# One transfer per tile for B and C of the small Mamba in a two-layer metaformer kernel

## The chip, the cores and the metric

The kernel runs on one core of one Trainium2 chip. The metric is the device time of one execution in microseconds (us). A version's time is the median of several executions.

## The reference, cut to what matters

The input is 8 images of 256 channels and 32 x 32 pixels, so 1,024 tokens each. Two layers follow one another: a large Mamba block and a mixture of experts, then a block of depthwise convolutions with a small Mamba, and a feed-forward on the best half of the tokens.

```python
# layer 0
x = x + vim_block(ln_c(x))            # Mamba, 512 inner channels, 16 states
t = t + moe(ln_t(t))                  # 8 experts, the best 2 of each token
# layer 1
x_mb = x[:, 224:256]                  # 32 channels go to the small Mamba
x = x + concat(x_id, conv3x3, conv1x11, conv11x1, mamba(x_mb))
t = t + ffn_on_top_half(ln_t(t))
```

The small Mamba has 64 inner channels and 16 states for each image. With u, delta, B and C computed from the tokens, it runs along the 1,024 tokens:

```python
dA  = exp(delta[..., None] * A)                       # A: 64 channels x 16 states
dBu = delta[..., None] * B[:, :, None, :] * u[..., None]
h = h * dA_t + dBu_t                                  # for each token t
y = sum(h * C_t[:, None, :], axis=-1)
```

B and C have one value for each image, token and state. They are the same for all 64 channels of an image, and differ between images.

## The kernel before, in words

**Tiling.** Channels lie on the 128 partitions, tokens on the free axis, in halves of N = 512 tokens. The large Mamba has 512 inner channels, so four blocks of 128; it runs as 16 units (8 images by 2 halves of the tokens). The small Mamba has only 64 channels, so two images share the partitions: image 0 of the pair has partitions 0 to 63, image 1 has 64 to 127. Eight images make four groups, and each group runs the small Mamba once (`mamba_in`, `mamba_scan`, `mamba_out`).

**One pair of states.** `scan_pair` (L777) does two states of one half for 128 channels, in this order: GpSimd multiplies delta times u by B of both states (L780, tile `dbu`); ScalarE makes the decay (L785); VectorE scans along the tokens (L788) and multiplies by C (L793); where a pair is marked, GpSimd adds the two states (L797); TensorE adds the products into the accumulator `y` (L804). The large Mamba needs 512 such pairs in all, the small one 64 (4 groups by 8 pairs of states by 2 halves).

**B and C.** For each pair, B of two states is one tile `bc` of 128 partitions x 2 x 512 f32 (512 KB), and C is another. There are four `bc` buffers for both Mambas (`"bc": tiles("bc", wide2, 4)`, L467), taken strictly in the order of the planned priorities. A buffer is free again once its reader has gone: L780 for B, the second L793 for C. The values come from a DRAM tile `rows`. In the large Mamba (L839) one DMA on SyncE's queue spreads two rows over all 128 partitions. In the small Mamba the two images need different rows: `rows` of one half has 64 rows of 512 values, first 32 for image 0 (16 of B, 16 of C), then 32 for image 1. The function `fetch` (L1413) therefore issues two DMAs for one tile, one for each image and half of the partitions.

**What sets the order.** Nothing runs in the order of the source. Each piece of work is a `Step` with an engine, an estimated cost and a priority. `Flow.run` (L206) is a list scheduler that runs while the program is built: it simulates the engines with these costs, picks steps by priority, and so fixes the order of the instructions on each engine, SyncE's DMA queue too. Buffers are assigned as the plan reaches them. `dma` (L203) makes a step on SyncE of `us` microseconds (0.4 unless said otherwise) whose data comes 2.3 + KB/180 us later. On the chip each engine follows its fixed order and waits on semaphores only. While TensorE is expected to be idle, `warm` (L522) puts filler matmuls there (L525).

**Beside the small Mamba.** The small Mambas of groups 0 to 2 lie among the large Mamba's last units, experts of other groups, and the feed-forward. Their loads stand in the same queue: expert weights (L1127, `we`, three buffers), rows of experts (L1088, `xb`), stores (L1187), tokens in and out (L904, L1617, L1645).

Of the kernel before, what the change touches and what calls it, by code (L numbers as in the profile page):

```python
# [38 lines left out]
N = 512  # L39
KC = C // P  # L40
DI0, DI1, DS, DR0 = 512, 64, 16, 16
# [131 lines left out]
class Flow:  # L173
# [29 lines left out]
    def dma(self, prio, kb, run, reads=(), writes=(), fills=(), claims=(), us=0.4):  # L203
        return self.step(SP, us, prio, run, reads, writes, fills, claims, lat=2.3 + kb / 180)
# [94 lines left out]
def layers(g, ctx, x, a, out):  # L299
    tc, nc = g.tc, g.nc  # L300
# [142 lines left out]
    step, dma = flow.step, flow.dma  # L443
# [54 lines left out]
    def buf(name, line=None):  # L498
        b = Buf(pool[name], line)
        if line is not None:  # L500
            line.bufs.append(b)
        return b
# [270 lines left out]
    def paired(i, sp):  # L773

        return (sp + 1) * PAIRED[i] // (DS // 2) > sp * PAIRED[i] // (DS // 2)

    def scan_pair(prio, dts, dtxs, n, bt, ct, y, scales, initial, last, stop, paired):  # L777

        dbu = buf("dbu")
        gpsimd(2.45, prio, lambda: nc.gpsimd.tensor_tensor(  # L780
            dbu.v, dtxs.v[:, n : n + 1].to_broadcast(wide2), bt.v, ALU.mult), [dtxs, bt], [dbu], scan=True)
        for j in range(2):

            h = buf("da")
            step(ACT, 0.69, prio, lambda j=j, h=h: nc.scalar.activation(  # L785
                h.v, dts.v[:, n], AF.Exp, scale=scales(j)), [dts], [h], table="exp", scan=True)
            at = [] if initial is None else [initial[0]]
            step(DVE, 1.25, prio, lambda j=j, h=h: nc.vector.tensor_tensor_scan(  # L788
                h.v, h.v, dbu.v[:, j], 0.0 if initial is None else initial[1](j), ALU.mult, ALU.add),
                [dbu, *at], [h], scan=True)  # L790
            if last is not None:
                step(ACT, 0.19, prio, lambda j=j, h=h: nc.scalar.copy(last[1](j), h.v[:, N - 1 :]), [h], fills=[last[0]])  # L792
            step(DVE, 0.68, prio, lambda j=j, h=h: nc.vector.tensor_tensor(  # L793
                dbu.v[:, j], h.v, ct.v[:, j], ALU.mult), [h, ct], [dbu], scan=True)

        if paired:
            gpsimd(1.3, prio + 2.3, lambda: nc.gpsimd.tensor_tensor(  # L797
                dbu.v[:, 0], dbu.v[:, 0], dbu.v[:, 1], ALU.add), [], [dbu])

        def sums():  # L800
            if stop and n == 0:
                live[0] = None
            for j in range(1 if paired else 2):
                nc.tensor.matmul(  # L804
                    y.v[:, n], g.ident, dbu.v[:, j], start=False, stop=stop and (paired or j == 1)
                )

        step(PE, 0.9 if paired else 1.8, prio + 2.5, sums, [dbu], [y], scan=True)

    def start_y(y, skips, xs, prio):  # L810
        def go(n):
            nc.tensor.matmul(y.v[:, n], skips[n], xs.v[:, n], start=True, stop=False)
            if n == 0:
                live[0] = y

        for n in range(2):
            step(PE, 0.9, prio, lambda n=n: go(n), [xs], fills=[y])

    def end_y(y, sz, prio):
        for n in range(2):  # L820
            step(DVE, 0.72, prio, lambda n=n: nc.vector.tensor_tensor(
                sz.v[:, n], sz.v[:, n], y.v[:, n], ALU.mult), [y], [sz])
# [581 lines left out]
    def mamba_scan(n, pos):  # L1404
        grp = groups[n]
        state, y = buf("state1"), buf("y")
        start_y(y, [skip1, skip1], grp["xs"], pos)
        for sp in range(DS // 2):
            for hf in range(2):
                both = buf("bc"), buf("bc")  # L1410
                for j in range(2):

                    def fetch(j=j, hf=hf, sp=sp, both=both):  # L1413
                        for i in range(2):
                            at = i * 2 * DS + j * DS + 2 * sp
                            nc.sync.dma_start(
                                both[j].v[i * DI1 : (i + 1) * DI1],
                                grp["rows"][hf].v[at : at + 2].partition_broadcast(DI1),
                            )

                    dma(pos + 2 * sp + hf - 6, 512, fetch, [grp["rows"][hf]], [both[j]], us=0.8)
                scan_pair(
                    pos + 2 * sp + hf, grp["dt"], grp["dtx"], hf, *both, y,
                    lambda j, sp=sp: neg_a1[:, 2 * sp + j : 2 * sp + j + 1],
                    (state, lambda j, sp=sp: state.v[:, 2 * sp + j : 2 * sp + j + 1]) if hf else None,
                    None if hf else (state, lambda j, sp=sp: state.v[:, 2 * sp + j : 2 * sp + j + 1]),
                    sp == DS // 2 - 1, paired(len(units) + n, sp),
                )
        end_y(y, grp["sz"], pos + DS)
# [235 lines left out]
    for i, s in enumerate(UNIT_AT):  # L1665
        if i == 0:
            unit_prep(0)
        dt_of(i, 1, s + 4)
        if i + 1 < len(units):
            fetch_x(i + 1, s)  # L1670
        scan_unit(i, s)
        if i + 1 < len(units):
            unit_prep(i + 1)
        end = s + 2 * DS
        tokens(i, end + 1)
        if i % 4 == 3:
            n = i // 4
            at = PLAN[n]
            route(n, end + 12)
            scatter(n, end + 16, at["put"])  # L1680
            experts(n, *at["experts"])
            combine(n, *at["combine"])
            taps_of(n, *at["taps"])
            m = at["mamba"]
            mamba_in(n, m - 26, m + 5)
            mamba_scan(n, m)
            mamba_out(n, m + DS + 2)
            assemble(n, *at["assemble"])
            ranks(n, at["ranks"])
            feed_forward(n, *at["ffn"])  # L1690
            finish(n, *at["finish"])
# [146 lines left out]
```

## Time and profile before

| What | Value |
|---|---|
| median of 3 executions | 3852.95 us (3839.76 to 3853.16) |
| the profiled execution, its own time | 3870.05 us |
| span from first to last instruction | 3868.2 us, granted TensorE clock 0.940 |
| large Mamba's `bc` DMAs (L839) | 512, issued from 51.0 to 2874.4 us |
| small Mamba's `bc` DMAs (L1416) | 256, issued from 2328.9 to 3642.3 us |
| the four small Mambas, first to last L1416 issue | 2328.9 to 2430.0, 2856.8 to 2985.3, 3263.5 to 3378.6, 3535.6 to 3642.3 us |
| length of these four windows | 101.1, 128.5, 115.1, 106.7: 451.4 us |

An engine's busy time is the time in which it runs instructions. The DMA share is the mean share of time in which each of the core's 16 DMA engines had a packet in hand, and a packet here is mostly one run of up to 4,096 bytes into one partition. "L780 <- DMA bc<-rows" in a table of waits means that the instruction of line 780 had an idle engine before it until a transfer into `bc` had landed. DMA instructions on SyncE's queue (SPq) have a duration too, that of their issue, not of their transfer.

### The profile page before, as it was taken

What the parts mean: (1) busy time and instruction counts of PE and PEld (TensorE: products, weight loads), DVE (VectorE), ACT (ScalarE), POOL (GpSimd) and SP (SyncE); (2) the same over time, 40 slices, a digit from 0 to 9 for tenths busy, and PEclk for the clock granted to TensorE, in tenths of its full rate; (3) what the DMA queues carried; (4) which work ended last, traced back from release to release, by engine and by line L of the source; (5) the groups of instructions that cost most, each with busy time, mean ns of one, the idle gap of its engine ahead of it and who ended that gap; (6) DMA issues with size and microseconds to landing.
All of it is one profiled execution on the core that took longest, in us unless ns stands there. A gap on an engine that the chain in (4) does not pass through costs nothing. (4 is left out here: it accounts for less than half of the span.)

```text
span 3868.2 us, 38209 instructions
## 1 busy us (share of the span) xinstructions
PE 3299.0 (85%) x10818; PEld 1849.4 (48%) x10818; DVE 2978.3 (77%) x4281; ACT 2207.2 (57%) x4010; POOL 2327.8 (60%) x1587
## 2 busy tenths in 40 slices
PE   8888888788889888978997798988987889799768
PEld 3333333333544444434553444554555666566446
DVE  4899899989679978976898898779787527557751
ACT  4555565465757557645765665665764456556433
POOL 3567567588577768866775886545765433424522
PEclk9999999999999999998999999999888989899989
DMA  6333333344544435535553558654669666967955
GB/s 232 122 123 131 114 131 132 106 151 162 200 139 167 165 129 194 181 111 172 172 174 122 195 181 226 204 184 136 200 204 223 222 213 214 243 215 215 247 175 168
DMA packets 277073, 676.67 MB, mean 175 GB/s; under 512 B 33063, under 2 KB 114349, under 8 KB 276862
## 3 DMA queue, kind: packets, MB, share of 16 engines
q1 hardware_dynamic: 258430, 623.88, 51.2%
q0 software_dynamic: 18432, 50.36, 4.1%
q8 instruction: 87, 1.43, 0.2%
q14 instruction: 124, 1.02, 0.1%
HBM read 572.92 MB, written 101.19 MB: 174 GB/s over the span
## 5 line engine op out<-in xcount | busy, mean ns | idle before, releaser
L780 POOL TENSOR_TENSOR dbu<-dtx,bc 128x1024 f32<-128x1024 f32 x576 | 1359.3, 2368 | 515.6 <-PE y L804 349.0
L804 PE MATMUL y<-dbu,ident 128*128 128x512 f32 x1564 | 822.6, 635 | 217.9 <-POOL dbu L797 185.7
L785 ACT ACTIVATE mm<-dt,neg_a 128x512 f32<-128x512 f32 x1152 | 770.3, 688 | 208.2 <-DVE dbu L793 190.4
L788 DVE TENSOR_TENSOR_SCAN mm<-mm,dbu 128x512 f32<-128x512 f32 x576 | 703.9, 1222 | 229.7 <-ACT mm L785 153.8
L793 DVE TENSOR_TENSOR dbu<-mm,bc 128x512 f32<-128x512 f32 x1152 | 796.4, 691 | 81.4 <-DMA bc<-rows 18.0
L788 DVE TENSOR_TENSOR_SCAN mm<-mm,state,dbu 128x512 f32<-128x512 f32 x576 | 738.2, 1282 | 59.5 <-POOL dbu L780 38.7
L797 POOL TENSOR_TENSOR dbu<-dbu 128x512 f32<-128x512 f32 x370 | 480.9, 1301 | 299.4 <-DVE dbu L793 291.3
L804 PEld LDWEIGHTS y<-dbu,ident 128*128 128x128 f32 x1564 | 281.6, 197 | 560.5 <-POOL dbu L797 278.7
L1179 PE MATMUL mm<-we,hid 128*128 128x256 f32 x1984 | 486.4, 398 | 36.0 <-ACT state L792 13.0
L792 ACT COPY state<-mm 128x1 f32<-128x1 f32 x576 | 91.4, 160 | 731.6 <-DVE dbu L793 710.9
L1157 PE MATMUL mm<-xbt,we 128*128 128x256 f32 x1984 | 474.3, 391 | 30.4 <-DMA we<-in_W12f 10.4
L1179 PEld LDWEIGHTS mm<-we,hid 128*128 128x128 f32 x1984 | 387.8, 199 | 156.3 <-issue 47.4
L1157 PEld LDWEIGHTS mm<-xbt,we 128*128 128x128 f32 x1984 | 383.4, 196 | 139.2 <-issue 46.9
L525 PE MATMUL y<-still 128*128 128x512 bf16 x1059 | 275.7, 395 | 0.0
L721 PE MATMUL mm<-pre,w_tap 128*128 128x512 f32 (+3 forms) x512 | 240.8, 612 | 28.6 <-ACT pre L708 27.3
L440 ACT ACT_TABLE_LOAD x176 | 225.8, 1283 | 3.1
L1250 POOL DMA_INDIRECT ys<-slots_y,slot x128 | 122.2, 954 | 160.0 <-PE mm L1262 69.0
L1163 ACT ACTIVATE hid<-mm,we 128x256 f32<-128x256 f32 x496 | 196.8, 475 | 37.8 <-PE mm L1157 29.1
L525 PEld LDWEIGHTS <-still 128*128 128x128 bf16 x1059 | 105.9, 101 | 192.6 <-issue 118.8
L721 PEld LDWEIGHTS mm<-pre,w_tap 128*128 128x128 f32 x512 | 95.5, 193 | 166.8 <-issue 103.9
L1068 POOL DMA_INDIRECT slots_x<-xg,slot x128 | 129.8, 1014 | 68.4 <-DVE acc_b L1323 31.2
L1621 POOL DMA_INDIRECT ys<-y,slot_t x64 | 63.1, 986 | 158.7 <-DVE xc L1631 59.0
(251 smaller groups left out, 3983.6 us busy)
## 6 DMA issues: line engine op xcount, KB each, us to landing
bc<-rows SPq DMA_DIRECT2D x512, 512.0 KB
bc<-rows SPq DMA_DIRECT2D x256, 256.0 KB
we<-in_W SPq DMA_DIRECT2D x92, 514.0 KB
we<-in_W SPq DMA_DIRECT2D x92, 512.0 KB
xb<-slots_x SPq DMA_DIRECT2D x92, 256.0 KB
slots_y<-xo SPq DMA_DIRECT2D x92, 256.0 KB
we<-in_W12f SPq DMA_DIRECT2D x32, 514.0 KB
xc<-x SPq DMA_DIRECT2D x64, 256.0 KB
```

Source lines behind the costliest of these rows:

```text
L440: nc.scalar.preload_act_table_set(tables[name])
L525: nc.tensor.matmul(live[0].v[:, 0], still, wide, start=False, stop=False)
L721: nc.tensor.matmul(tc_.v[:, cut:], w_tap[:, c, j], pre.v[:, cut + j : j + N], start=j == 3, stop=j == 0)
L780: gpsimd(2.45, prio, lambda: nc.gpsimd.tensor_tensor(dbu.v, dtxs.v[:, n : n + 1].to_broadcast(wide2), bt.v, ALU.mult), [dtxs, bt], [dbu], ...
L785: step(ACT, 0.69, prio, lambda j=j, h=h: nc.scalar.activation(h.v, dts.v[:, n], AF.Exp, scale=scales(j)), [dts], [h], table="exp", scan=True)
L788: step(DVE, 1.25, prio, lambda j=j, h=h: nc.vector.tensor_tensor_scan(h.v, h.v, dbu.v[:, j], 0.0 if initial is None else initial[1](j), AL ...
L793: step(DVE, 0.68, prio, lambda j=j, h=h: nc.vector.tensor_tensor(dbu.v[:, j], h.v, ct.v[:, j], ALU.mult), [h, ct], [dbu], scan=True)
L797: gpsimd(1.3, prio + 2.3, lambda: nc.gpsimd.tensor_tensor(dbu.v[:, 0], dbu.v[:, 0], dbu.v[:, 1], ALU.add), [], [dbu])
L804: nc.tensor.matmul(y.v[:, n], g.ident, dbu.v[:, j], start=False, stop=stop and (paired or j == 1))
L1157: nc.tensor.matmul(tv[:, f], we[0].v[:, at : at + P], xbt.v[:, k], start=k == 0, stop=k == KC - 1)
L1163: nc.scalar.activation(hid.v[:, f], tv[:, f % 2], func, bias=we[0].v[:, at : at + 1])
L1179: nc.tensor.matmul(to, hid.v[:, f, h * P : (h + 1) * P], we[1].v[:, f * C : (f + 1) * C], start=extra is None and f == 0, stop=f == FC - 1,)
```

## The change

`fetch` issues one DMA per `bc` tile. Its source is a view of `rows` with a leading dimension of two images, then a dimension of 64 that repeats with step zero, then the two rows; its destination is the whole tile of 128 partitions. The estimated cost of the step falls from 0.8 to 0.4 us, so the planner sees the same bytes with a shorter issue. Nothing else is edited; what the lower estimate does to the order of the other instructions is the planner's doing.

```diff
                     def fetch(j=j, hf=hf, sp=sp, both=both):
-                        for i in range(2):
-                            at = i * 2 * DS + j * DS + 2 * sp
-                            nc.sync.dma_start(
-                                both[j].v[i * DI1 : (i + 1) * DI1],
-                                grp["rows"][hf].v[at : at + 2].partition_broadcast(DI1),
-                            )
-
-                    dma(pos + 2 * sp + hf - 6, 512, fetch, [grp["rows"][hf]], [both[j]], us=0.8)
+
+                        rows = grp["rows"][hf].v.rearrange("(i m) n -> i m n", i=2)
+                        at = j * DS + 2 * sp
+                        nc.sync.dma_start(
+                            both[j].v, rows[:, at : at + 2].unsqueeze(1).to_broadcast([2, DI1, 2, N]))
+
+                    dma(pos + 2 * sp + hf - 6, 512, fetch, [grp["rows"][hf]], [both[j]])
```

In the built program the new DMA has the destination pattern 128 partitions x 1 x 1,024 values and the source pattern 2 (step 32 rows) x 64 (step 0) x 1,024 values. Each old one had 64 partitions x 1,024 values on the destination and 64 (step 0) x 1,024 on the source. The new line is L1417.

## The prediction

> **What bounds the kernel now.** I began with the page's first two parts, to see whether one engine sets the time.
>
> ```profile
> span 3868.2 us, 38209 instructions
> ...
> PE 3299.0 (85%) x10818; PEld 1849.4 (48%) x10818; DVE 2978.3 (77%) x4281; ACT 2207.2 (57%) x4010; POOL 2327.8 (60%) x1587
> ```
>
> None does over the whole span: TensorE's 85% contains 1,059 filler matmuls (275.7 us at L525), and VectorE has 77%. So the change must be judged inside the four windows in which the small Mambas fetch B and C. The table by windows sets them beside a stretch of the large Mamba (200 to 400 us). Its columns are length, busy time of each engine, granted clock, DMA share, GB/s.
>
> ```profile
> core 0: us, PE busy (x) PEld busy (x) DVE busy (x) ACT busy (x) POOL busy (x), PEclk, DMA share, GB/s
> 200.00:400.00 200.00, 172.29 (x473) 76.34 (x473) 186.57 (x226) 106.85 (x173) 138.47 (x74) 0.95 0.39 129
> 2328.90:2430.00 101.10, 84.22 (x254) 44.04 (x253) 79.86 (x97) 57.73 (x96) 61.94 (x39) 0.95 0.85 216
> 2856.80:2985.30 128.50, 105.65 (x368) 71.30 (x365) 95.96 (x117) 66.07 (x118) 70.56 (x39) 0.88 0.86 220
> 3263.50:3378.60 115.10, 88.69 (x332) 62.90 (x331) 59.34 (x63) 68.96 (x117) 50.61 (x30) 0.90 1.01 247
> 3535.60:3642.30 106.70, 80.25 (x300) 48.49 (x298) 86.45 (x80) 66.30 (x115) 68.93 (x45) 0.92 0.98 264
> ```
>
> In the large Mamba VectorE is the bound (186.57 of 200 us) and the DMA engines are 39% busy. In the small Mamba's windows VectorE falls to 52 to 81%, and the DMA engines are 85 to 100% busy, at only 216 to 264 GB/s. The view of one source line says who waits for these transfers:
>
> ```profile
> L1416 SPq DMA_DIRECT2D bc<-rows x256: 444/498/995, 2328.9 to 3642.3; - x128
> ...
>   POOL dbu L780: 115.8, 35
>   DVE dbu L793: 18.0, 14
> ```
>
> GpSimd's multiply by B waited 115.8 us for them and VectorE's multiply by C 18.0 us, of 451.4 us of windows. So these windows are bound by DMA. The DMA view of the third window says how full the queue is:
>
> ```profile
> DMA packets 11236, 28.46 MB, mean 247 GB/s; under 512 B 1520, under 2 KB 5104, under 8 KB 11231
> ...
> q1 hardware_dynamic: 11039, 27.87, 99.6%
> ```
>
> 99.6% x 16 x 115.1 us over 27.87 MB is 15.2 bytes per ns and engine. In 200 to 400 us the same view has 38.5% for 25.75 MB: 20.9. In the trace's list of packets, those of 4,096 bytes take a median of 159 ns and a mean of 186 between 100 and 300 us. In the four windows their medians are 264 to 280 ns and their means 251 to 280 (together 263). The same bytes are slower when they go to half the partitions.
>
> [...] No view of the profile names the engine of a packet, and the trace of before has no transfer with such a mismatch. Its w_dt load of 17 rows (L345) does raise its semaphore in only two steps, at 4.25 and 10.43 us, where a tile of 128 rows shows 16[...].
>
> **The change part by part.**
>
> *Split over engines.* The old transfers have 64 on both sides[...]. The new source starts with 2 images, the new destination with 128 partitions. [...] each of two engines takes 64 packets, and the other 14 take none. I take this. The other bound is k = 16, a gain, worked out among the rivals.
>
> *Engine time of the two.* One tile is 64 packets x 159 ns = 10.2 us on each of the two engines. One small Mamba has 32 tiles: 325.6 us; all four 1,302 us. [...] I take the trace's undisturbed 159 ns with little on it: 165 ns, 1,352 us. Bounds: 156 ns, the shortest in the list for this size (1,278 us), and 186 ns, the large Mamba's mean (1,524 us).
>
> *What else stands on the two engines.* [...] In the order built from the changed kernel, between first and last L1417 issue of the four groups stand other SyncE transfers of 5.0, 10.0, 13.0 and 9.3 MB, 37.3 MB. A sixteenth is 2.33 MB, at 4,096 bytes per 159 ns 90 us.
>
> *Do the two engines ever run dry?* B's buffer returns after a multiply of 2.35 us (L780) and C's after about 2.7 us (L788 and L793 at 1.28 and 0.69 us, with waits), while three tiles or more, 30 us, are still queued. So the Mamba's own loop keeps them full. What can empty them is the work in between: an expert's weights land only when their sixteenth on the two slow engines has passed, up to 30 us later; ScalarE (L1163) and SyncE (L1127, L1187) wait for them or for what follows from them, and behind them in their fixed orders stand the exponentials of L785 and the next L1417. Before, the engines idled 15% of 101.1, 14% of 128.5 and 2% of 106.7 us, some 35 us. I keep this 35 us, since the same waits now lie beside longer transfers; bounds zero and a quarter more on the windows (360 us).
>
> *Sum.* The windows become 1,352 + 90 + 35 = 1,477 us instead of 451.4: +1,026 us. All other engines fit beneath: PE's busy time in the four windows is 358.8 us, VectorE's 321.6. Their order is fixed, so work after the windows cannot come forward to fill the 14 idle engines' time. Cover that I lean on: that other transfers of the windows, 90 us, add to the time and are not hidden; were they all in gaps, 90 us less.
>
> *Issue on SyncE.* 256 issues of 498 ns (127 us) become 128. The large Mamba's single transfer issues in 320 ns; the new one at 320 to 500 ns costs 41 to 64 us. The 63 to 86 us saved lie beside transfers that are late anyway: nothing. Without that cover it could be worth no more than those 86 us. A wait is not added, but what stands behind the new L1417 in the queue is: weights, rows and stores behind tiles of 10 us.
>
> *Order.* The built orders agree until the first small Mamba (some 910 rows of SyncE's queue), then differ almost everywhere; filler matmuls go from 1,059 to 1,112, in planned gaps. I count zero, with 20 us either way, the width at which a re-plan without another cause would be lost.
>
> Own time: 3870 + 1026 = 4896 us. The profiled execution lies 17 us above the median shown (3852.95), so a median of about **4,880 us**.
>
> **The rivals.**
>
> *A, all 16 engines (ends faster).* [...] The place is the generation of the packets for L1417; the point from which it decides is the number of engines. Before, each engine carried 256 such packets per group, 256 x 263 ns = 67 us; with k engines it is 4,096/k x 159 ns = 651/k us: equal near k = 10. With 16 the packets fall from 263 to 186 ns: 16,384 x 77 ns / 16 = 79 us less in windows that are full: 3853 - 79 = 3,774 us, and at most the 134 us of waits, 3,719. For it: the windows are bound by DMA, and the large Mamba's fetch of 128 partitions shows 186 ns. Against it: the leading 2 of the source[...].
>
> *B, two engines and broken overlap (slower still).* The packets take 186 ns (1,524 us), the rest 90 us, and the waits of experts behind 30 us of queue leave the two engines idle a fifth of the time: (1,524 + 90) / 0.8 = 2,018 us for the windows, +1,566, 5,419 us. For it: three weight buffers and four of `bc`, one fixed order. Against it: the two engines have over 25 us of stock per wait, and in the third window of before, with 8 stores and 15 weight loads, the engines never idled.
>
> *C, nothing moves.* Sixteen engines, but the windows at once bound by TensorE (358.8 busy of 451.4 us) and its order, or by the new plan: 3,853 us. For it: in window three POOL waits for PE too. Against it: 44.8 us of waits there are for `bc`.
>
> **How the numbers follow.** Two engines with overlap kept: 0.82, time 4,880, own range 4,700 (1,278 us of packets, 25 us of all else) to 5,200 (1,524 + 90, and some 185 us idle). B above 5,200: 0.06. A: 0.09. C: 0.03. The range 4,700 to 5,200 thus leaves out 0.18. About 0.5%, 19 us, is what a measurement of this kernel can tell from no change. Faster 0.09, same 0.03, slower 0.88.
>
> **What would show it.** Right: four windows of 300 us or more; in them a DMA share near 2/16 plus a little, 0.15 to 0.25, at some 60 to 90 GB/s; GpSimd's L780 waiting for `bc` about 800 to 1,200 us in total; tiles 10 us apart; 4,096-byte packets back near 159 ns. A would show windows below 105 us at a share under 0.8. B would show windows over 450 us with weights (`we`) as a large wait. Wrong on the size: packets of two engines other than 159 to 186 ns, or windows much longer than the packets on two engines fill. If L1416's successor shows shares above 0.5, the step on the split has failed.

## The result and the profile after

The changed kernel takes 4839.81 us (median, 4833.67 to 4846.90), the kernel before 3846.84 us beside it. The ratio is 1.258, 95% interval 1.255 to 1.262: 993 us slower. The profiled execution took 4833.67 us.

The page's first part: no engine works longer in any way that would explain 964 us of span. VectorE and GpSimd do the same work; TensorE's busy time rises by 111 us. 97 of them lie in the four windows below, over nearly the same number of matmuls (1,266 against 1,254), and there the granted clock was 0.64 to 0.67 where it had been 0.88 to 0.95.

```profile
span 4832.0 us, 38122 instructions
...
PE 3410.5 (71%) x10877; PEld 1900.2 (39%) x10877; DVE 2946.0 (61%) x4281; ACT 2212.0 (46%) x4013; POOL 2321.6 (48%) x1589
```

The table by windows, for the same stretch of the large Mamba and for the four windows from first to last L1417 issue. Columns: length, busy time of PE, PEld, DVE, ACT, POOL, granted clock, DMA share, GB/s.

```profile
200.00:400.00 200.00, 172.78 (x474) 76.70 (x475) 186.51 (x229) 107.53 (x176) 139.75 (x75) 0.95 0.39 129
2326.30:2645.10 318.80, 113.77 (x255) 54.27 (x253) 77.70 (x96) 58.51 (x96) 59.59 (x37) 0.64 0.18 66
3102.30:3439.70 337.40, 122.97 (x343) 77.42 (x341) 89.85 (x109) 62.55 (x109) 68.42 (x38) 0.67 0.21 77
3732.10:4073.30 341.20, 119.72 (x364) 83.00 (x362) 59.16 (x62) 73.03 (x123) 48.79 (x29) 0.66 0.24 84
4253.60:4587.00 333.40, 99.45 (x304) 57.24 (x302) 76.29 (x81) 66.21 (x116) 64.50 (x43) 0.65 0.23 82
```

The large Mamba is untouched. The four windows have grown from 451.4 to 1,330.8 us, and the DMA share in them has fallen from between 85 and 101% to between 18 and 24%, at a third of the GB/s. Others wait for this queue, and yet its engines are busy a fifth of the time: that points to few engines. A quiet stretch inside the first window shows it bare:

```profile
GB/s 47 51 57 49 49 49 57 90 49 49 49 49 57 49 57 49 49 49 49 57 49 57 49 49 49 49 57 57 49 49 49 49 49 57 57 49 49 49 49 49
DMA packets 265, 1.04 MB, mean 52 GB/s; under 512 B 4, under 2 KB 16, under 8 KB 264
...
q1 hardware_dynamic: 264, 1.03, 12.7%
```

12.7% of 16 engines is two engines, all the time. In this stretch the packets of 4,096 bytes take 162 ns in the trace's list, median and mean: 25.3 GB/s each, 51 for two. The same list says how many packets were in flight, that is started and not yet ended, at each moment. Over the four windows it was exactly two in 1,061 of 1,331 us, more in 264, and fewer in only 5.

The view of the new line shows who waits, and something about the issue:

```profile
L1417 SPq DMA_DIRECT2D bc<-rows x128: 482/3922/12114, 2326.3 to 4587.0; - x128
...
  POOL dbu L780: 1089.0, 63
  DVE dbu L793: 436.0, 58
```

The waits for B have grown from 115.8 to 1,089.0 us, those for C from 18.0 to 436.0. The timeline of a stretch shows the rhythm: B lands every 20 us, C 10 us after it (columns: start, duration, engine, line).

```profile
2561.43 2.34 POOL L780 TENSOR_TENSOR dbu<-dtx,bc 128x1024 f32<-128x1024 f32 x1 [17.70 <-DMA bc<-rows]
...
2571.58 0.69 DVE L793 TENSOR_TENSOR dbu<-mm,bc 128x512 f32<-128x512 f32 x1 [6.55 <-DMA bc<-rows]
...
2581.76 2.34 POOL L780 TENSOR_TENSOR dbu<-dtx,bc 128x1024 f32<-128x1024 f32 x1 [17.87 <-DMA bc<-rows]
...
2591.91 0.69 DVE L793 TENSOR_TENSOR dbu<-mm,bc 128x512 f32<-128x512 f32 x1 [6.49 <-DMA bc<-rows]
```

SyncE's own timeline, in the last window: an issue that took a third to a half of a us before can now hold the queue for about 10. A row with x2 is two issues and what lies between them.

```profile
4329.04 11.54 SPq L1127 DMA_DIRECT2D we<-in_W12f  x2
4340.63 1.96 SPq L1417 DMA_DIRECT2D bc<-rows  x1
4342.68 10.66 SPq L1644 DMA_DIRECT2D out<-xo  x1
4353.39 2.30 SPq L1088 DMA_DIRECT2D xb<-slots_t  x1
4355.80 9.65 SPq L1417 DMA_DIRECT2D bc<-rows  x2
```

Whatever stands behind a tile is held too, weights and output stores among them. That left two theories of the slowdown. *Number of engines*: the leading 2 of the source confines every tile to the same two engines, and the long issues are only the queue backing up behind them. *Form of the source*: a source of this form makes the issue itself take some 10 us, and the data would flow if it were issued sooner.

### The profile page after: what moved, and what is told of

The parts are those of the page before. It is cut to its first block, busy times and chain, and to the rows that moved or that the text cites. A ratio compares the mean times of both kernels' runs of the same rounds, so it can differ in the third digit from the quotient of the medians.

```text
span 4832.0 us, 38122 instructions
## 1 busy us (share of the span) xinstructions
PE 3410.5 (71%) x10877; PEld 1900.2 (39%) x10877; DVE 2946.0 (61%) x4281; ACT 2212.0 (46%) x4013; POOL 2321.6 (48%) x1589
## 5 line engine op out<-in xcount | busy, mean ns | idle before, releaser
L780 POOL TENSOR_TENSOR dbu<-dtx,bc 128x1024 f32<-128x1024 f32 x576 | 1355.8, 2362 | 1466.6 <-DMA bc<-rows 1109.2
L804 PE MATMUL y<-dbu,ident 128*128 128x512 f32 x1564 | 852.9, 655 | 521.3 <-POOL dbu L797 446.5
L793 DVE TENSOR_TENSOR dbu<-mm,bc 128x512 f32<-128x512 f32 x1152 | 796.5, 691 | 501.8 <-DMA bc<-rows 436.0
L1157 PE MATMUL mm<-xbt,we 128*128 128x256 f32 x1984 | 497.0, 404 | 205.5 <-DMA we<-in_W 126.1
L1179 PE MATMUL mm<-we,hid 128*128 128x256 f32 x1984 | 505.7, 409 | 115.7 <-DMA we<-in_W 57.0
L1157 PEld LDWEIGHTS mm<-xbt,we 128*128 128x128 f32 x1984 | 399.9, 204 | 322.5 <-issue 186.7
L1179 PEld LDWEIGHTS mm<-we,hid 128*128 128x128 f32 x1984 | 399.9, 206 | 243.1 <-issue 120.0
L525 PE MATMUL y<-still 128*128 128x512 bf16 x1112 | 293.9, 398 | 0.0
L1142 PE MATMUL mm<-ident,xb 128*128 128x128 f32 x432 | 73.5, 297 | 164.3 <-DVE dbu L793 58.4
L882 PE MATMUL mm<-w_out,sz 128*128 128x264 f32 x512 | 137.6, 415 | 68.1 <-ACT state L792 42.5
```

Of the source, the lines that this page charges most:

```text
L525: nc.tensor.matmul(live[0].v[:, 0], still, wide, start=False, stop=False)
L780: gpsimd(2.45, prio, lambda: nc.gpsimd.tensor_tensor(dbu.v, dtxs.v[:, n : n + 1].to_broadcast(wide2), bt.v, ALU.mult), [dtxs, bt], [dbu], ...
L804: nc.tensor.matmul(y.v[:, n], g.ident, dbu.v[:, j], start=False, stop=stop and (paired or j == 1))
L1157: nc.tensor.matmul(tv[:, f], we[0].v[:, at : at + P], xbt.v[:, k], start=k == 0, stop=k == KC - 1)
L1179: nc.tensor.matmul(to, hid.v[:, f, h * P : (h + 1) * P], we[1].v[:, f * C : (f + 1) * C], start=extra is None and f == 0, stop=f == FC - 1,)
```

## The experiments

All of them change only lines of the small Mamba. "Windows" are as above, from its first to its last fetch of each group, summed over the four. Packet times are means over all packets of 4,096 bytes in the windows, group by group, from the trace's list. Each ratio is to the kernel before on the same chip.

### More engines by more copies of the rows: e1_k4, e2_k8, e3_k16

The rows of B and C are written c times to DRAM (c = 2, 4, 8), so that the source can start with 2c. With c = 8 it is 16 x 8 x 1,024 values.

```diff
-        "rows": tiles("rows", [4 * DS, N], 4, where=g.dram),
+        "rows": tiles("rows", [8 * 4 * DS, N], 4, where=g.dram),
...
-            dma(prio + 5, 128, lambda dbl=dbl, rw=rw: nc.sync.dma_start(rw.v, dbl.v[2 * DS : m6]), [dbl], [rw])
+            def spread(dbl=dbl, rw=rw):
+                to = rw.v.rearrange("(i q m) n -> i m q n", i=2, q=8)
+                for i in range(2):
+                    at = 2 * DS * (1 + i)
+                    nc.sync.dma_start(to[i], dbl.v[at : at + 2 * DS].unsqueeze(1).to_broadcast([2 * DS, 8, N]))
...
-                        rows = grp["rows"][hf].v.rearrange("(i m) n -> i m n", i=2)
+                        rows = grp["rows"][hf].v.rearrange("(i m) n -> i m n", i=16)
...
-                            both[j].v, rows[:, at : at + 2].unsqueeze(1).to_broadcast([2, DI1, 2, N]))
+                            both[j].v, rows[:, at : at + 2].unsqueeze(1).to_broadcast([16, P // 16, 2, N]))
```

> Each row of B and C of the small Mamba is written twice to DRAM, so that the source of the one transfer per tile starts with 4 instead of 2; same planned order as the changed kernel. Theory (number of engines): 4 engines carry a tile, 32 packets x 162 ns = 5.2 us instead of 10.4; 128 tiles save 663 us: about 4180 us, 102 GB/s in stretches where only these tiles move. Rival (the form of the source makes the issue on SyncE's queue slow, some 10 us for each tile whatever the leading number): still about 4840 us.

Measured: 4208.21 us, ratio 1.094 (1.090 to 1.098). The windows sum to 760.7 us. A quiet stretch in the second half of its first window has twice the rate and twice the share:

```profile
DMA packets 566, 2.04 MB, mean 102 GB/s; under 512 B 20, under 2 KB 84, under 8 KB 565
...
q1 hardware_dynamic: 565, 2.04, 25.6%
```

Four engines, all the time. The median issue of the line falls from 3.9 to 0.55 us although the source still has three dimensions with a repeat in the middle, so the form is not what made it long: the second theory falls. It is also the same four for every tile: two tiles were issued 0.6 us apart, at 2476.8 and 2477.4 us, and between 2478 and 2490 us four packets were in flight for 11 of 12 us, never more than six.

> As e1_k4 with four copies of each row, so that the source starts with 8. Theory (number of engines): 2.6 us for a tile on each of 8 engines, 83 us for a small Mamba, so the transfers are about as fast as the halves of the kernel before (67 us on each of 16 engines): 3840 to 3920 us. Rival (form of the source): still about 4840 us.

Measured: 3970.92 us, ratio 1.032 (1.029 to 1.035); windows 530.3 us. Above what I expected: my 83 us for a small Mamba counted undisturbed packets and left out the other transfers. The mean packet here took 202 to 218 ns. 128 tiles x 16 packets x 210 ns is 430 us. With the other transfers, 90 us by the prediction's estimate and up to 119 if their packets are as long, that makes 520 to 550: eight engines still set the windows. The packets in flight agree: exactly eight for 222 of the 530 us, and two to seven together for 20.

> As e1_k4 with eight copies of each row, so that the source starts with 16. Theory (number of engines): all 16 engines and all 128 partitions, packets of 160 to 190 ns, 41 to 48 us of engine time for a small Mamba; the windows are no longer bound by these transfers: 3740 to 3830 us, DMA share below 0.7 in the windows. Rival (form of the source): still about 4840 us. [...]

Measured: 3864.58 us, ratio 1.0055 (1.0038 to 1.0073); windows 434.2 us. Nearly the whole loss is gone (a ratio of 1.258 has become 1.0055), as the number of engines says, but it is no faster than before. The packets took 241 to 267 ns, as slow as before, and the third window shows full engines:

```profile
DMA packets 11638, 29.68 MB, mean 254 GB/s; under 512 B 1074, under 2 KB 5095, under 8 KB 11631
...
q1 hardware_dynamic: 11439, 29.07, 91.2%
```

So 16 engines and 128 partitions do not by themselves bring the short packets of the large Mamba. Which of three things does it: the new order, the eightfold stores, or this split?

### No copies, one image for all: e4_one_image

```diff
-                        rows = grp["rows"][hf].v.rearrange("(i m) n -> i m n", i=2)
+                        rows = grp["rows"][hf].v
...
-                            both[j].v, rows[:, at : at + 2].unsqueeze(1).to_broadcast([2, DI1, 2, N]))
+                            both[j].v, rows[at : at + 2].partition_broadcast(P))
```

> One transfer per tile that spreads the rows of image 0 of each pair over all 128 partitions: the second image of each pair gets the first one's B and C, and nothing is copied in DRAM. Same planned order as the changed kernel. Both theories expect a fast transfer here: 3730 to 3820 us; theory (number of engines) expects e3_k16 within 20 us of it, the rival some 1000 us away from it.

Measured: 3802.17 us, ratio 0.987 (0.984 to 0.990); windows 394.9 us, packets 192 to 195 ns. So one transfer per tile can be faster than the two of before, even in this order. e3_k16 stands 62 us above it, not within 20.

### The order alone and the transfer alone: e5_order_only, e6_transfer_only

```diff
-                    dma(pos + 2 * sp + hf - 6, 512, fetch, [grp["rows"][hf]], [both[j]], us=0.8)
+                    dma(pos + 2 * sp + hf - 6, 512, fetch, [grp["rows"][hf]], [both[j]])
```

> The kernel before with only the estimated cost of the step lowered from 0.8 to 0.4 us: two transfers per tile in the planned order of the changed kernel. Theory: the order is worth next to nothing, 3825 to 3865 us, so all of the 996 us come from the transfer. Rival (the new order hides a loss, which would also explain why e3_k16 is not faster): 3865 to 3900 us.

Measured: 3873.63 us, ratio 1.0059 (1.0030 to 1.0087). That lies in the rival's range: the order costs about 23 us. It is part of the answer to e3_k16, whose ratio in this order, 1.0055, is the same as with the old halves: its one transfer gained nothing over them. The profiled executions cannot show where the 23 us lie, since they differ by 2 us only (3871.83 and 3870.05); e8 and e9 below can.

```diff
-                    dma(pos + 2 * sp + hf - 6, 512, fetch, [grp["rows"][hf]], [both[j]])
+                    dma(pos + 2 * sp + hf - 6, 512, fetch, [grp["rows"][hf]], [both[j]], us=0.8)
```

> The changed transfer with the estimated cost left at 0.8 us, so in the planned order of the kernel before. Theory: 4810 to 4870 us, as the changed kernel. If the lower estimate made the plan overcommit the queue: under 4750 us.

Measured: 4842.55 us, ratio 1.259 (1.253 to 1.264), as the changed kernel. The whole loss is the transfer. The interval is some 20 us wide either way, so what the order adds or takes beside two saturated engines was not resolved.

### The form of e3_k16 without its stores: e7_blocks

```diff
-                        rows = grp["rows"][hf].v.rearrange("(i m) n -> i m n", i=2)
+                        rows = grp["rows"][hf].v
...
-                            both[j].v, rows[:, at : at + 2].unsqueeze(1).to_broadcast([2, DI1, 2, N]))
+                            both[j].v, rows[at : at + 32].rearrange("(q r) n -> q r n", r=2).unsqueeze(1).to_broadcast([16, 8, 2, N]))
```

> One transfer per tile whose source has 16 blocks, each two rows further on in the DRAM tile, repeated over 8 partitions; no copies are made, and the partitions get other rows of B and C than they should. It has e3_k16's form of source without e3_k16's stores. Theory P (a source of 16 x 8 hands each engine 8 neighbouring partitions[...]): packets of 4,096 bytes at 240 to 270 ns on average in the windows as in e3_k16, 3825 to 3860 us. Theory S (the eightfold store of the rows is what e3_k16 lost): packets near 195 ns as in e4_one_image, 3790 to 3815 us.

Measured: 3861.25 us, ratio 1.0023 (1.0005 to 1.0041); windows 430.4 us, packets 249 to 274 ns. By the ratios that is 0.3%, some 12 us, under e3_k16, which may be the price of its stores. The third window:

```profile
DMA packets 11230, 28.89 MB, mean 251 GB/s; under 512 B 1066, under 2 KB 5107, under 8 KB 11224
...
q1 hardware_dynamic: 11032, 28.30, 92.7%
```

So the slow packets come with the 16 x 8 form and not with the stores.

### Images interleaved on the partitions: e8_interleaved, e9_interleaved_old_order, e10_interleaved_halves

The weights of the small Mamba are permuted so that image 0 has the even and image 1 the odd partitions. The source of one transfer then starts with the 64 repeats.

```diff
+    perm = np.arange(P).reshape(2, DI1).T.reshape(-1)
...
-        "w_out1": twice(c1["out_proj_w"].T),
-        "ch1": np.concatenate([ch1, ch1]),
+        "w_out1": twice(c1["out_proj_w"].T)[perm],
+        "ch1": np.concatenate([ch1, ch1])[perm],
...
-                            both[j].v, rows[:, at : at + 2].unsqueeze(1).to_broadcast([2, DI1, 2, N]))
+                            both[j].v, rows[:, at : at + 2].unsqueeze(0).to_broadcast([DI1, 2, 2, N]))
```

> The channels of the two images are interleaved on the partitions (image 0 on even, image 1 on odd ones) by permuting the small Mamba's weights, so that the source of one transfer per tile is 64 (step 0) x 2 images and starts with 64. Same planned order as the changed kernel. Theory (number of engines): [...] no slowdown: 3790 to 3860 us; 3790 to 3815 with packets near 195 ns if engines get the partitions as in a plain transfer to 128, 3825 to 3860 with packets near 260 ns if they get neighbouring ones. Rival (only a source that is one dimension over the partitions is spread): 4840 us.

Measured: 3816.45 us, ratio 0.991 (0.988 to 0.995), in the order that costs 23 us on its own; 57 us under e5_order_only. Packets 193 to 204 ns, windows 393.6 us. The third window carries about as many bytes as e7_blocks's at a lower share:

```profile
DMA packets 11174, 28.72 MB, mean 283 GB/s; under 512 B 1061, under 2 KB 5091, under 8 KB 11168
...
q1 hardware_dynamic: 10976, 28.12, 81.7%
```

With the estimate put back to 0.8 us, which gives the order of before:

> e8_interleaved with the estimated cost of the step put back to 0.8 us, so one transfer per tile on 16 engines in the planned order of the kernel before. Theory (transfer and order add up): e8_interleaved's ratio 0.9911 over e5_order_only's 1.0059, 0.985, some 3795 us. Rival (the order's loss is tied to the half transfers): as e8_interleaved, 3810 to 3820 us.

Measured: 3795.59 us, ratio 0.986 (0.983 to 0.989), 52 us under the kernel before: the transfer's gain and the order's loss add up. Its profiled execution is 23 us shorter than e8_interleaved's, with windows of the same length (394.4 and 393.6 us). The three stretches between the windows make the difference: they are 6.8, 12.1 and 4.0 us shorter. So the order's loss appears to lie there (the two ran on different chips); no single wait was found for it. The four windows, to be set against those of before:

```profile
2337.60:2427.90 90.30, 80.95 (x246) 41.95 (x245) 79.78 (x97) 56.91 (x95) 61.77 (x37) 0.98 0.75 242
2856.60:2965.60 109.00, 92.41 (x355) 64.11 (x354) 97.95 (x116) 65.32 (x118) 69.53 (x38) 0.94 0.77 262
3232.70:3325.70 93.00, 83.10 (x330) 59.94 (x329) 58.49 (x62) 68.30 (x117) 50.22 (x30) 0.96 0.88 308
3477.00:3579.00 102.00, 81.50 (x297) 49.48 (x296) 81.98 (x80) 64.29 (x114) 70.83 (x45) 0.88 0.84 276
```

And who waits for the line now:

```profile
L1417 SPq DMA_DIRECT2D bc<-rows x128: 512/524/847, 2337.6 to 3579.0; - x128
...
  POOL dbu L780: 53.1, 29
  DVE dbu L793: 3.7, 3
```

B's waits halve to 53.1 us and C's nearly go.

e10 keeps the interleaving and the two transfers per tile of the kernel before (`both[j].v[i::2]` for `both[j].v[i * DI1 : (i + 1) * DI1]`).

> Images interleaved on the partitions as in e8_interleaved, but two transfers per tile again, one to the even and one to the odd partitions, in the planned order of the kernel before. [...] near 195 ns in the windows, 3790 to 3820 us. If engines get neighbouring partitions of the 64 [...]: 240 to 270 ns, 3835 to 3870 us.

Measured: 3805.75 us, ratio 0.990 (0.987 to 0.993); packets 175 to 209 ns, windows 399.2 us. So the two transfers per tile were not the fault in the kernel before. Their place was: in the same order, with the same two transfers, 64 neighbouring partitions give 251 to 280 ns, every second of 128 gives 175 to 209. e9's one transfer is at most slightly better than e10's two, since the intervals overlap.

### What the split hands to an engine: e11_32_blocks, e12_128_sources

```diff
-                        rows = grp["rows"][hf].v.rearrange("(i m) n -> i m n", i=2)
                         at = j * DS + 2 * sp
+                        row = grp["rows"][hf].v[at : at + 2]
                         nc.sync.dma_start(
-                            both[j].v, rows[:, at : at + 2].unsqueeze(1).to_broadcast([2, DI1, 2, N]))
+                            both[j].v.rearrange("p k n -> p (k n)"),
+                            bass.AP(tensor=row.tensor, offset=row.offset, ap=[[N, 32], [0, 4], [1, 2 * N]]))
```

e12 has `[[N // 4, P], [1, 2 * N]]` in place of the last pattern.

> As e7_blocks, but the source has 32 blocks, each one row further on, repeated over 4 partitions[...]; the partitions again get other rows than they should. If engines get two neighbouring blocks: as e7_blocks, packets at 240 to 275 ns, 3845 to 3875 us. If they get blocks that lie apart, as e8_interleaved and e10_interleaved_halves suggest: near 195 ns, 3800 to 3825 us.

Measured: 3805.14 us, ratio 0.988 (0.985 to 0.992); packets 185 to 195 ns, windows 397.0 us.

> One transfer per tile with a source of one dimension of 128, each partition's 4,096 bytes starting 512 bytes further on in the DRAM tile; the partitions again get other values than they should. If e3_k16 and e7_blocks were slow because their engines read different addresses: packets at 240 ns or more, 3845 us or more. If it was the share of partitions that each engine writes: near 195 ns, 3790 to 3825 us, as e4_one_image.

Measured: 3789.16 us, ratio 0.987 (0.983 to 0.990); packets 185 to 192 ns, windows 391.0 us. Different addresses do not slow the reads here: 185 to 192 ns with 128 of them against 192 to 195 in e4_one_image. Sixteen blocks of 8 partitions are slow (241 to 274 ns in e3_k16 and e7_blocks), 32 blocks of 4 are not (185 to 195). Why is not shown: the trace names no engine, so it was not seen which partitions each one writes.

## Why the prediction was right, point by point

**The split.** Right. The step put k, the number of engines that carry one transfer, at 2 for a source that starts with 2. The trace of before has no transfer of this form, so that was my assumption; the runs show it. Two engines at 51 GB/s, four at 102 in e1_k4, and the whole loss gone with 16 (e3_k16, e7_blocks, e8_interleaved) agree. For sources that start with 2, 4 and 8 the commonest number of packets in flight was exactly that: two in 1,061 of 1,331 us of windows, four in 483 of 761, eight in 222 of 530. Which of the 16 engines these are, no run here shows.

**Engine time.** 165 ns for a packet was assumed, and 162 was measured where nothing else moved: 8,192 packets on each of the two engines x 162 ns are 1,327 us against the predicted 1,352.

**The rest of the windows.** Predicted 90 us for other transfers, my estimate from a sixteenth of their bytes on each engine, and 35 us idle. No run measures that sixteenth by itself. The windows grew by 879.4 us and the rest of the span by 84.3, together 963.7. The rest grew mostly because the last tiles of a group land after its last issue: the last multiply by C that waited for a tile began 27 to 36 us after that issue, where before it was 1.2 us at most. 451.4 + 963.7 - 1,327 leaves 88 us for both terms. Fewer than two packets were in flight for only 5 us of the windows, so the two engines hardly ever ran dry, and 35 us was too much: together with the packets (25 us) this makes the 62 us between the predicted +1,026 of own time and the measured 964. Some 29 of these 62 us are the spread of executions: the profiled one of before lies 23 us above its median, the one after 6 below, and the medians differ by 993. Rival B did not occur. PE waited for weights, 126.1 us at L1157 for `we` from `in_W`, as B foresaw, but the two engines were at work meanwhile.

**Issue on SyncE.** The conclusion (nothing) held, the working did not. I counted on 41 to 64 us for the new issues; they took 595 us, and SyncE's DMA issues in all 1,634 us against 658. They lie beside packets that kept the two engines at work, and the sum above has no room for a further cost. That the term was nothing was right for another reason than the one given.

**Order.** Put at zero, 20 us either way. e5_order_only shows 23 us slower with the transfers of before (12 to 33 by its interval), at or just outside that bound; beside the slow transfers e6_transfer_only does not resolve it.

**Rival A.** It did not occur, and its working was short of one condition. It took 16 engines on 128 partitions to be enough for packets of 186 ns. e3_k16 and e7_blocks have both and stay at 241 to 274. The 186 ns also came from a stretch with the DMA engines 39% busy and the 263 from one at 85 to 101%, so the two figures differ in load as well as in partitions. e10_interleaved_halves settles that: its packets are short at 237 to 311 GB/s in the windows, where before moved 216 to 264. The right form gains 57 us (e8_interleaved against e5_order_only) to 52 us (e9 against before), where 79 was put down for it: with e9's packets at 181 to 206 ns the windows come near TensorE's work, 338.0 of 394.3 us, which may be why.

**Marks set out beforehand.** Windows of 300 us or more: 318.8 to 341.2. Share 0.15 to 0.25: 0.18 to 0.24. 60 to 90 GB/s: 66 to 84. L780's waits 800 to 1,200 us: 1,089. Tiles 10 us apart: 10.

## What to carry to other kernels

Before two DMAs become one, write down the first dimension of the source's pattern: a view that is one tidy array in the program, here 2 images x 64 repeats, put every tile on two of 16 engines, and sources that start with 4 and 8 used four and eight. The sign of it in the profile was a low DMA share (0.18 to 0.24) with L780 waiting 1,089 us for DMA, and the rate was a small multiple of one engine's 25 GB/s: 51 on two, 102 on four. Where two halves need different data, interleave them over the partitions rather than stack them; that alone was worth 1 to 1.4% here, with one transfer per tile or with two.

## What the runs showed of the hardware that I had not expected

- SyncE's DMA instruction held its queue when the engines were far behind: with two engines saturated an issue of a tile took 3.9 us in the median and up to 12.1, against 0.5 with 16 engines (e8_interleaved; in e9_interleaved_old_order too, where the tile landed 5.5 us after its issue began). The DMAs behind it in the queue started later, tiles and other transfers alike: in the last window the store of L1644 (`out`), begun at 4342.68 us, took 10.66 us to issue, and the load of L1088 (`xb`) behind it began only at 4353.39.
- All 128 partitions in one transfer did not by themselves bring short packets. A source of 16 blocks x 8 partitions has packets of 241 to 274 ns (e3_k16, e7_blocks); 32 x 4, 64 x 2 and 128 x 1 have 181 to 206.
- A transfer to 64 partitions is not slow as such: every second partition gave packets of 175 to 209 ns (e10_interleaved_halves), as good as all 128 in e8_interleaved and e9_interleaved_old_order (181 to 206); 64 neighbouring ones gave 251 to 280 before. I had put that down to the number 64. Why the place of the partitions matters, and why the 16 x 8 form is slow although it writes to all 128, no trace here shows.
